# A new order of the work and a fourth place for the inner sums in a two-layer graph network on one core

## The chip, the cores and the metric

The kernel runs on one core of a Trainium2 chip. The core's engines are TensorE (PE in the profile; its weight loads are shown apart as PEld), VectorE (DVE), ScalarE (ACT), GpSimd (POOL) and SyncE (SP), whose queue issues nearly all the transfers here. The metric is the device time of one execution in microseconds (us). A single run is named with its own time, several runs with their median.

## The reference, cut to what matters

There are 128 graphs of 128 nodes with 512 features each, and two layers. All is float32.

```python
deg  = sum(adj, -1, keepdims=True)                      # layer 0
agg  = einsum('bij,bjf->bif', adj, x) / maximum(deg, 1e-6)
x    = layernorm(x + relu(concat([x, agg], 2) @ W.T))

Xw   = x @ Wv + bv                                      # layer 1
sj, si = Xw @ aw[:d, 0], Xw @ aw[d:, 0]
a    = adj * exp(leaky_relu(sj[:, None, :] + si[:, :, None] + ab, 0.2))
T    = a / (sum(a, -1, keepdims=True) + 1e-12)
H    = (x @ Wk[0] + bk[0]) + T @ ((x @ Wk[1] + bk[1]) + T @ (x @ Wk[2] + bk[2]))   # same sum, regrouped
out  = layernorm(x + relu(H))
```

(The reference writes H as a loop over k with powers of T; the kernel computes the nested form in the last line but one. How the biases of the second and first term pass through T is folded into constants made once at the start.)

## The kernel before

Work goes in groups of four graphs: 32 groups in layer 0, then 32 in layer 1. A group is a matrix of 512 rows by 512 features. It is multiplied by a wide matrix of weights (1024 columns in layer 0, 4 x 385 in layer 1, the two score columns among them) by a scheme of seven products in place of eight, used on two levels: seven outer products of seven inner ones each, so 49 products of 128x128 weights with 256 or 385 columns. The sums and differences that such a scheme needs are made by GpSimd on the left operands, and by VectorE and ScalarE when they take results out of the accumulators.

The accumulators are eight PSUM banks, `bA` and `bB`, in two lanes of four. An outer product takes a lane for seven steps. Seven steps of one outer product are chained: the first is copied to another bank (so the third, which adds to the same bank, must wait for that copy), the third is added to a saved sum (so the fifth must wait for that addition), and so on. To hide these waits the steps of two outer products, one in each lane, are interleaved.

Names of steps, as they stand in the strings of the program and in the text below: in layer 0 `P12`, `P56` and `P74` are pairs of outer products (a step is two products, 0.86 us), `t.1` to `t.7` are the inner steps of the last outer product and `t.8` to `t.11` the four products with the normalised adjacency; a small first letter (`p74`) means the group before. In layer 1 `O1` to `O7` are outer products (a step is one product of 385 columns, 0.65 us) and `c.1` to `c.8` are the T products of `combine` for the group before (0.86 us each, 512 columns); `x.1` to `x.8` are those of the very last group. Each graph b of a group has two T products. `one(b)` multiplies T with the third term, adds the second term (two VectorE additions, lines 829 and 830) and puts this inner sum into a place `v1s`, and then ScalarE copies the first term into the bank (line 831). `two(b)` multiplies T with the inner sum on top of that copy, and `residual` (line 380) takes the bank out, with ReLU, residual and the row sum for the layer norm. There are three places for inner sums.

The order is written by hand, or rather by tables. `PA`, `PB` and their like give the order of the steps on TensorE: `PF` for the first group, `PA` for a group of layer 0, `PT` and `PG` at the passage to layer 1, `PB` for a group of layer 1, `PL` for the last one. The tables `PLACES_...` give, for all other work (loads, transpositions, sums, layer norm, softmax, stores), the half step after which it is issued. A function issues its instructions where its place stands, and every engine runs its own instructions in that order, so the tables decide also what stands in front of what in the queues of VectorE, ScalarE, GpSimd and SyncE. Semaphores guard the data; an early place never makes a wrong result, and a late or a crowded one makes a wait.

Lines that the text needs: 155 (all products), 259 (transposition of the left operand, 0.6 to 0.7 us on VectorE), 400 and 401 (sums of `t.2`), 409 (sum of `t.5`), 599 and 601 (degree), 614 and 810 (transposition of the adjacency or of T), 626 (bias copied into a bank before `O5.1`), 637 and 676 (additions that the fifth and the seventh step of an outer product wait for), 504 and 517 (ScalarE's two passes of the layer norm), 725 to 734 (scores), 784 to 802 (softmax of the scores), 744 to 770 (the last group's softmax, which makes the row sums on TensorE and keeps T in place of the detour through memory that the other groups take).

```python
for f, b in ((one, 0), (one, 1), (one, 2), (two, 0), (one, 3), (two, 1), (two, 2)):
    f(b)
    yield
two(3)
```

Of the kernel before, what the change touches and what calls it, by code (L numbers as in the profile page):

```python
# [8 lines left out]
FP = mybir.dt.float32  # L9
# [7 lines left out]
def kernel(  # L17
# [15 lines left out]
    P = 128  # L33
# [25 lines left out]
    def need(*keys):  # L59
        for k in keys:  # L60
            assert k in done, k
# [10 lines left out]
    v1s = [big[:, 28 * BW + F * i : 28 * BW + F * (i + 1)] for i in range(3)]  # L72
# [78 lines left out]
    for t in bA + bB:  # L151
        nc.tensor.matmul(t, ident, ident[:, None, :].to_broadcast([P, Q, P]), start=True, stop=True)
# [603 lines left out]
    def end_rows(g, h):  # L756
        need(("end_scores", g), ("adj_turn",))
        T = TTs[g][:, 2 * h : 2 * h + 2].rearrange("p b n -> p (b n)")
        pt = lanes[0][1 + h][:, :FH]
        V.tensor_mul(T, T, adjs[2 * NG - 1][:, 2 * h : 2 * h + 2].rearrange("p b n -> p (b n)"))  # L760
        mm(pt, ones[:].to_broadcast([P, P]), T, True)

    def end_norm(g, h):
        need(("end_rows", g, h))
        T = TTs[g][:, 2 * h : 2 * h + 2].rearrange("p b n -> p (b n)")
        pt = lanes[0][1 + h][:, :FH]
        rr = halves()[:, :FH]
        V.tensor_scalar(rr, pt, ROW_EPS, None, ALU.add)
        V.reciprocal(rr, rr)  # L769
        V.tensor_mul(T, T, rr)  # L770
# [41 lines left out]
    def combine(lane, g):  # L812
        n = NG + g
        X, Y, W, Z = lane
        at_ = {0: X, 1: Z, 2: W, 3: Y}
# [8 lines left out]
        def one(b):  # L824
            need(("end_norm", g, b // 2) if g == NG - 1 else ("t_turn", g))
            need(("O4" if b > 1 else "O3", g, 7), ("sum_c", g, 0), ("sum_c", g, 1))
            mm(at_[b], TTs[g][:, b], row(b, 0, F, 0), True)
            v = v1[b] = v1s[(g * G + b) % 3]
            V.tensor_add(v[:, :258], at_[b][:, :258], row(b, F, 2 * BW, 0))
            V.tensor_add(v[:, 258:], at_[b][:, 258:], row(b, 0, 254, 1))  # L830
            L_.copy(at_[b], row(b, 254, 766, 1))  # L831

        def two(b):
            mm(at_[b], TTs[g][:, b], v1[b])
            late.append((residual, n, b, at_[b]))
        for f, b in ((one, 0), (one, 1), (one, 2), (two, 0), (one, 3), (two, 1), (two, 2)):
            f(b)
            yield
# [12 lines left out]
    def step(lane, name, g, k):  # L851
# [3 lines left out]
    PA = "p74.5 P12.1 P12.2 p74.6 P12.3 p74.7 P12.4 t.1 P12.5 P12.6 t.2 P12.7 P56.1 t.3 P56.2 t.4 t.5 P56.3 t.6 t.7 t.8 t.9 t.10 t.11 P74.1 P74.2 P56.4 P56.5 P56.6 P74.3 P56.7 P74.4".split()  # L855
    PT = "p74.5 p74.6 O1.1 O1.2 O1.3 p74.7 O1.4 t.1 O1.5 O1.6 t.2 O1.7 O2.1 t.3 O2.2 t.4 t.5 O2.3 t.6 t.7 t.8 t.9 t.10 t.11 O2.4 O2.5 O2.6".split()
    PG = ("O5.1 O5.2 O5.3 O5.4 O2.5 O2.6 O6.1 O6.2 O5.5 O5.6 O5.7 O7.1 O6.3 O6.4 O7.2 "
          "O6.5 O2.7 O7.3 O6.6 O7.4 O6.7 O4.1 O4.2 O7.5 O4.3 O7.6 O7.7 O4.4 c.1 O4.5 "
          "O4.6 c.2 c.3 c.4 O4.7 O3.1 O3.2 O3.3 O3.4 c.5 c.6 c.7 c.8 O3.5 O3.6").split()
    PB = ("O1.1 o3.7 O1.2 O1.3 O2.1 O1.4 O1.5 O1.6 O2.2 O1.7 O2.3 O2.4 O5.1 O5.2 O2.5 O5.3 O2.6 O5.4 O2.7 "  # L860
          "O6.1 O5.5 O6.2 O5.6 O6.3 O5.7 O6.4 O7.1 O6.5 O6.6 O7.2 O7.3 O6.7 O4.1 O7.4 O7.5 O4.2 O4.3 O7.6 "
          "O4.4 O4.5 O7.7 c.1 O4.6 O4.7 O3.1 O3.2 c.2 O3.3 c.3 c.4 c.5 c.6 c.7 c.8 O3.4 O3.5 O3.6").split()
    PL = ("O1.1 o3.7 O1.2 O2.1 O1.3 O2.2 O1.4 O1.5 O1.6 O1.7 O2.3 O2.4 O5.1 O2.5 O5.2 O2.6 O2.7 O5.3 O5.4 O6.1 O5.5 O6.2 "
# [44 lines left out]
    def place_op(n, pos, name, m, *a):  # L908
# [7 lines left out]
        ("ln_apply", -2, 3): 4, ("ln_var", -2, 0): -9, ("sum_c22", -2): -40, ("ln_scales", -2): -1, ("ln_mean", -2): -15,  # L916
        ("ln_var", -2, 2): -4, ("load_y", -2, 1): -27, ("ln_apply", -2, 2): 10, ("ln_var", -2, 1): -4,
        ("load_y", -2, 0): -31, ("x_s4", -1): -36, ("ln_var", -2, 3): -12, ("x_s1", -1): -66, ("a_load", -2): -65,
        ("a_turn", -2): -36, ("x_s3", -1): -52, ("y_store", -2, 1): 25, ("ln_apply", -2, 1): 15, ("x_turn", 0, 0, 1): -20,
        ("y_store", -2, 0): 32, ("ln_apply", -2, 0): 15, ("load_left", 0, 0): -49, ("ln_apply", -1, 3): 68, ("x_s2", 0): 28,  # L920
        ("x_turn", 0, 1, 1): -37, ("load_adj", 0): 154, ("ln_var", -1, 0): 58, ("sum_c22", -1): 21, ("ln_scales", -1): 62,
        ("ln_mean", -1): 48, ("x_turn", 0, 0, 0): -28, ("ln_var", -1, 2): 55, ("load_y", -1, 1): 38, ("load_y", -1, 0): 40,
        ("ln_var", -1, 1): 55, ("ln_apply", -1, 2): 70, ("x_s1", 0): 5, ("x_turn", 0, 1, 0): -39, ("a_load", -1): 7,
        ("x_turn", 1, 0, 1): 55, ("x_inner", 0, 0): -12, ("a_norm", -1): -23, ("ln_var", -1, 3): 58, ("degree", -1): -48,
        ("a_turn", -1): 27, ("x_s3", 0): 19, ("y_store", -1, 1): 95, ("ln_apply", -1, 1): 79, ("x_inner", 0, 1): -29,
        ("y_store", -1, 0): 100, ("ln_apply", -1, 0): 82, ("load_left", 1, 0): 9, ("x_s1", 1): 97, ("x_turn", 1, 0, 0): 41,
        ("x_s2", 1): 99, ("x_s4", 0): 80, ("load_left", 1, 1): -24, ("x_inner", 1, 1): 61, ("x_turn", 1, 1, 0): 32,
        ("x_s3", 1): 127, ("x_inner", 1, 0): 64, ("x_turn", 1, 1, 1): 47, ("x_s2", -1): -44,
    }
    PLACES_A = {  # L930
        ("x_s4", 0): 35, ("ln_apply", 0, 3): 131, ("x_s2", 1): 86, ("x_turn", 1, 1, 1): 33, ("ln_var", 0, 0): 124,
        ("sum_c22", 0): 87, ("ln_scales", 0): 126, ("w_slot", 0, 1): 24, ("ln_mean", 0): 113, ("x_turn", 1, 0, 0): 33,
        ("ln_var", 0, 2): 124, ("load_y", 0, 1): 100, ("ln_var", 0, 1): 118, ("load_y", 0, 0): 100, ("ln_apply", 0, 2): 134,
        ("x_s1", 1): 67, ("x_turn", 1, 1, 0): 28, ("a_load", 0): 73, ("x_inner", 1, 0): 51, ("a_norm", 0): 36,
        ("ln_var", 0, 3): 115, ("degree", 0): 17, ("load_left", 2, 1): 38, ("w_slot", 0, 0): 4, ("a_turn", 0): 90,
        ("x_s3", 1): 83, ("y_store", 0, 1): 157, ("ln_apply", 0, 1): 140, ("x_turn", 1, 0, 1): 42, ("x_inner", 1, 1): 36,
        ("load_adj", 1): 37, ("y_store", 0, 0): 161, ("ln_apply", 0, 0): 138, ("load_left", 2, 0): 78,
    }
    PLACES_B = {
        ("t_norm", 0): 154, ("sum_r", 0, 1): 81, ("load_y", 0, 0): 170, ("ln_var", 0, 3): 230, ("x_turn", 1, 0, 1): 19,  # L940
        ("t_back", 0): 165, ("x_s1", 1): 66, ("ln_scales", 0): 239, ("t_sums", 0): 149, ("x_turn", 1, 1, 1): 19,
        ("load_left", 2, 0): 82, ("ln_var", 0, 1): 227, ("y_store", 0, 0): 264, ("t_turn", 0): 187, ("ln_var", 0, 2): 224,
        ("sum_c", 0, 0): 109, ("ln_apply", 0, 2): 273, ("ln_apply", 0, 3): 257, ("x_inner", 1, 1): 53, ("ln_var", 0, 0): 235,
        ("t_exp", 0): 140, ("load_left", 2, 1): 70, ("ln_apply", 0, 1): 257, ("y_store", 0, 1): 278, ("x_s2", 1): 68,
        ("x_turn", 1, 1, 0): -5, ("x_s3", 1): 97, ("ln_apply", 0, 0): 242, ("t_load", 0): 123, ("t_scores", 0): 119,
        ("x_turn", 1, 0, 0): 14, ("sum_r", 0, 0): 86, ("x_s4", 0): 42, ("load_adj", 0): 103, ("load_y", 0, 1): 190,
        ("ln_mean", 0): 223, ("sum_c", 0, 1): 115, ("x_inner", 1, 0): 41,
    }
    PLACES_M = {
        ("ln_mean",): 212, ("ln_apply", 3): 234, ("ln_var", 1): 219, ("ln_apply", 0): 250, ("y_store", 0): 251,  # L950
        ("ln_apply", 2): 231, ("ln_var", 2): 225, ("ln_apply", 1): 235, ("ln_var", 3): 225, ("ln_scales",): 230,
        ("y_store", 1): 244, ("ln_var", 0): 227,
    }
    PLACES_L = {
        ("end_store", 2): 158, ("sum_c", 1): 72, ("sum_r", 0): 71, ("end_store", 0): 158, ("t_scores",): 105,
        ("end_var", 1): 134, ("sum_r", 1): 71, ("load_adj",): 96, ("load_y", 0): 47, ("end_apply", 1): 160,
        ("load_y", 1): 106, ("end_mean", 1): 128, ("end_rows", 0): 111, ("end_mean", 0): 127, ("end_rstd", 2): 132,
        ("end_store", 1): 160, ("end_apply", 2): 137, ("end_stats", 2): 129, ("end_store", 3): 162, ("end_scales",): 140,
        ("sum_c", 0): 76, ("end_rstd", 3): 149, ("end_apply", 0): 144, ("end_scores",): 106, ("end_rows", 1): 111,
        ("end_norm", 0): 111, ("end_stats", 3): 138, ("end_norm", 1): 111, ("end_apply", 3): 158, ("adj_turn",): 96,  # L960
        ("end_var", 0): 131,
# [118 lines left out]
```

## Time and profile before

| what | us |
|---|---|
| median of 3 runs | 2085.56 (2084.93 to 2086.3) |
| the profiled execution, its own time | 2083.08 |
| its span, first to last instruction | 2081.3 |
| a group of layer 0, start to start in the chain of waits (101.57 to 126.32) | 24.75 |
| a group of layer 1 (919.52 to 958.43) | 38.91 |
| TensorE busy from 60 to 790 | 730.00 of 730 |
| TensorE busy from 860 to 2040 | 1179.80 of 1180 |
| TensorE busy from 2051.00 to 2072.70, the last group's end | 16.80 of 21.70 |
| after the last product, to the end of the span | 8.60 |

A page of this profile shows busy time by engine, the chain of work that ended last, and groups of instructions. A view of waits adds up, for one engine, the idle time before its instructions and what ended it. A timeline gives start, duration, engine, line, operation, tiles (written <- read), shapes and, in brackets, idle time before the instruction and what ended it. Each float32 product stands there as two weight loads and two MATMUL records, one after the other.

### The profile page before, as it was taken

How to read it: one execution, taken by the hardware profiler on the slowest of the kernel's cores; microseconds unless marked ns; L12 is line 12 of the kernel's file. 1: busy time of each engine (PE TensorE's matmuls, PEld its weight loads, DVE VectorE, ACT ScalarE, POOL GpSimd, SP SyncE). 2: the span in 40 equal slices, each digit the busy share in tenths (PEclk: the TensorE clock that was granted, in tenths of full speed). 3: DMA queues.
4: the chain of work that ended last, by engine and by line, in shares of the span. 5: the costliest groups of instructions: out<-in, count | busy, mean ns of one | idle time of the engine just before them, and what ended most of it. 6: DMA issues, size and time to landing. Idle time of an engine off the chain costs nothing.

```text
span 2081.3 us, 25875 instructions
## 1 busy us (share of the span) xinstructions
PE 2062.5 (99%) x7096; PEld 1329.9 (64%) x7096; DVE 1525.8 (73%) x3414; ACT 1155.7 (56%) x2875; POOL 1377.7 (66%) x1263
## 2 busy tenths in 40 slices
PE   9999999999999999999999999999999999999997
PEld 6778888888878886555555555555555555555553
DVE  6777777777777777676776776776776776776766
ACT  2656666666666666355455455455455465465464
POOL 5877888887676776656656656656556556556552
PEclk9999999999999999999999999999999999999999
DMA  9776666666667776435434535535535435435423
GB/s 206 174 190 194 180 182 179 160 187 192 163 160 190 190 183 218 107 87 122 116 87 115 124 87 127 112 87 128 111 87 130 109 87 132 107 87 132 107 67 117
DMA packets 431070, 287.13 MB, mean 138 GB/s; under 512 B 155593, under 2 KB 353865, under 8 KB 430924
## 3 DMA queue, kind: packets, MB, share of 16 engines
q1 hardware_dynamic: 429996, 284.15, 54.6%
q10 hardware_dynamic: 800, 1.31, 0.3%
q8 instruction: 56, 0.92, 0.2%
q14 instruction: 90, 0.74, 0.1%
q0 software_dynamic: 128, 0.01, 0.0%
HBM read 191.60 MB, written 93.79 MB: 137 GB/s over the span
## 4 chain that ended last, share of the span: by engine, by line
PE 97%; DVE 1%; DMA 1%; ACT 0%; issue 0%; POOL 0%; SPq 0%; ACTq 0%; DVEq 0%
PE bA L155 51%; PE bB L155 46%; DMA yd<-y 0%; DMA xb<-in_x_dram 0%; DMA y<-in_x_dram 0%; PE bA L181 0%; DVE s L769 0%; DVE y L380 0%; POOL r L709 0%; ACT y L517 0%; DVE big L995 0%; DVE xl L259 0%; DVE xu L259 0%; DVE big L1003 0%; SPq L83 0%
## 5 line engine op out<-in xcount | busy, mean ns | idle before, releaser
L155 PE MATMUL bB<-big,xu 128*128 128x385 f32 (+1 forms) x1806 | 569.5, 435 | 1.0 <-DVE c L676 0.7
L155 PEld LDWEIGHTS bB<-big,xu 128*128 128x128 f32 x1806 | 339.4, 190 | 166.6 <-issue 30.1
L155 PE MATMUL bA<-big,xl 128*128 128x256 f32 (+1 forms) x1358 | 395.9, 416 | 0.3 <-DVE bA L475 0.3
L155 PE MATMUL bB<-big,xs 128*128 128x256 f32 (+1 forms) x1316 | 388.8, 416 | 0.0
L155 PEld LDWEIGHTS bA<-big,xl 128*128 128x128 f32 x1358 | 256.8, 189 | 100.1 <-issue 15.5
L155 PEld LDWEIGHTS bB<-big,xs 128*128 128x128 f32 x1316 | 249.5, 190 | 84.2 <-issue 1.7
L155 PE MATMUL bA<-big,xu 128*128 128x256 f32 (+1 forms) x896 | 290.0, 435 | 0.2
L155 PE MATMUL bA<-c,TT 128*128 128x512 f32 x512 | 245.9, 592 | 3.0 <-DVE c L669 1.9
L504 ACT ACTIVATE junk<-y,mv 128x512 bf16<-128x512 f32 x252 | 181.3, 719 | 72.7 <-POOL mv L499 68.5
L155 PEld LDWEIGHTS bA<-big,xu 128*128 128x128 f32 x896 | 165.4, 189 | 82.2 <-DVE bA L637 9.7
L517 ACT ACTIVATE y<-y,mv,rstd 128x512 f32<-128x512 f32 x252 | 201.5, 812 | 1.4 <-POOL mv L512 1.4
L380 DVE SCALAR_TENSOR_TENSOR y<-bA,y 128x512 f32<-128x512 f32 x256 | 170.4, 683 | 19.6 <-PE bA L155 13.4
L155 PE MATMUL bA<-big,xs 128*128 128x385 f32 x448 | 178.3, 492 | 0.0
L709 POOL TENSOR_TENSOR r<-r,s 128x770 f32<-128x770 f32 x64 | 115.1, 1820 | 86.4 <-DVE c L669 86.4
L155 PE MATMUL bB<-big,xl 128*128 128x385 f32 (+1 forms) x462 | 167.2, 480 | 0.5 <-ACT bA L456 0.4
L155 PEld LDWEIGHTS bA<-c,TT 128*128 128x128 f32 x512 | 96.8, 189 | 93.0 <-issue 48.1
L790 POOL TENSOR_TENSOR T<-ag,T 128x512 f32<-128x512 f32 x31 | 39.5, 1275 | 175.9 <-ACT T L785 175.9
L499 POOL TENSOR_SCALAR mv<-mv 128x4 f32<-128x4 f32 x63 | 14.5, 230 | 212.3 <-DVE y L380 212.3
L270 POOL TENSOR_TENSOR xs<-xl 128x896 f32<-128x896 f32 x63 | 131.4, 2086 | 23.9 <-PE bB L155 23.9
L282 POOL TENSOR_TENSOR xu<-xu,xs 128x896 f32<-128x896 f32 x63 | 131.8, 2091 | 8.8 <-PE bB L155 8.8
L831 ACT COPY bA<-r 128x512 f32<-128x512 f32 x64 | 37.7, 590 | 176.4 <-DVE big L830 170.7
L637 DVE TENSOR_TENSOR bB<-bB,s 128x385 f32<-128x385 f32 x128 | 72.5, 567 | 85.1 <-PE bB L155 75.4
(190 smaller groups left out, 3636.7 us busy)
## 6 DMA issues: line engine op xcount, KB each, us to landing
xb<-in_x_dram SPq DMA_DIRECT2D x256, 128.0 KB, 3.8
y<-in_x_dram SPq DMA_DIRECT2D x64, 512.0 KB, 4.3
yd<-y SPq DMA_DIRECT2D x64, 512.0 KB, 3.0
xb<-yd SPq DMA_DIRECT2D x256, 128.0 KB, 5.8
y<-yd SPq DMA_DIRECT2D x64, 512.0 KB, 5.9
out_dram<-y SPq DMA_DIRECT2D x62, 512.0 KB, 2.8
ag<-in_adj_dram SPq DMA_DIRECT2D x63, 256.0 KB, 5.9
sb<-sd SPq DMA_DIRECT2D x252, 64.0 KB, 3.2
```

The lines of the kernel that those rows point to most:

```text
L155: nc.tensor.matmul(dst, lhsT, rhs, start=start, stop=True, skip_group_check=True)
L270: S_.tensor_add(xs[n][:, 0], xl[n][:, 0], xl[n][:, 1])
L282: S_.tensor_sub(xu[n][:, 1], xu[n][:, 1], xs[n][:, 1])
L380: V.scalar_tensor_tensor(y, t, 0.0, y, ALU.max, ALU.add, accum_out=mvs[n][:, b, 0:1])
L499: S_.tensor_scalar(mvs[n][:, :, 0], mvs[n][:, :, 0], -1.0 / F, None, ALU.mult)
L504: L_.activation(junk, ys[n, b // 2][:, b % 2], AF.Square, bias=mvs[n][:, b, 0:1], accum_out=mvs[n][:, b, 1:2])
L517: L_.activation(y, y, AF.Identity, bias=mvs[n][:, b, 0:1], scale=rstds[n][:, b : b + 1])
L637: V.tensor_add(W, X, s5)
L709: S_.tensor_add(r, r, s)
L790: S_.tensor_mul(T, adjs[NG + g], T)
L831: L_.copy(at_[b], row(b, 254, 766, 1))
```

## The change

1. `v1s` has a fourth place, a tile of its own, and each graph has its own place. In `combine` all four `one` stand ahead of the four `two`, in all groups but the last, where the order stays as it was.
2. The last group. The row sums of its softmax are made as columns: four products with a vector of ones in place of two with a matrix of ones. The reciprocal is then taken of two numbers in each row in place of 256, spread to a diagonal, and brought back to all rows by a product with ones. For three of its four graphs the first term is no longer copied by ScalarE: a product with the identity puts it into a bank of the other lane ahead of time (`end_base`), and the second T product goes there.
3. One of the eight warm-up products at the start is left out.
4. The strings `PA`, `PT`, `PG`, `PB` and `PL`, and all tables of places apart from that of the start, have new values.

```diff
-    v1s = [big[:, 28 * BW + F * i : 28 * BW + F * (i + 1)] for i in range(3)]
+    v1s = [big[:, 28 * BW + F * i : 28 * BW + F * (i + 1)] for i in range(3)] + [const.tile([P, F], FP, name="v1x")]
...
-    for t in bA + bB:
+    for t in bA + bB[:3]:
...
     def end_rows(g, h):
-        need(("end_scores", g), ("adj_turn",))
+        need(("end_scores", g), ("adj_turn",), *[("end_rows", g, 0)] * h)
+        T, pt = TTs[g], lanes[0][0]
+        t2 = T[:, 2 * h : 2 * h + 2].rearrange("p b n -> p (b n)")
+        V.tensor_mul(t2, t2, adjs[2 * NG - 1][:, 2 * h : 2 * h + 2].rearrange("p b n -> p (b n)"))
+        for b in (2 * h, 2 * h + 1):
+            mm(pt[:, b : b + 1], T[:, b], ones, b == 0)
+
+    def end_recip(g, h):
+        need(("end_rows", g, 1))
+        t = lanes[0][0][:, 2 * h : 2 * h + 2]
+        rr = small.tile([P, 2], FP, name="rr2")
+        V.tensor_scalar(rr, t, ROW_EPS, None, ALU.add)
+        V.reciprocal(rr, rr)
+        if h == 0:
+            ends["dr"] = p1.tile([P, G, N], FP, name="dr", tag="sb")
+        for b in (0, 1):
+            V.tensor_scalar(ends["dr"][:, 2 * h + b], ident, rr[:, b : b + 1], None, ALU.mult)
+
+    def end_norm(g, h):
+        need(("end_recip", g, 1), *[("end_norm", g, 0)] * h)
         T = TTs[g][:, 2 * h : 2 * h + 2].rearrange("p b n -> p (b n)")
-        pt = lanes[0][1 + h][:, :FH]
-        V.tensor_mul(T, T, adjs[2 * NG - 1][:, 2 * h : 2 * h + 2].rearrange("p b n -> p (b n)"))
-        mm(pt, ones[:].to_broadcast([P, P]), T, True)
-
-    def end_norm(g, h):
-        need(("end_rows", g, h))
-        T = TTs[g][:, 2 * h : 2 * h + 2].rearrange("p b n -> p (b n)")
-        pt = lanes[0][1 + h][:, :FH]
-        rr = halves()[:, :FH]
-        V.tensor_scalar(rr, pt, ROW_EPS, None, ALU.add)
-        V.reciprocal(rr, rr)
-        V.tensor_mul(T, T, rr)
+        pt = lanes[0][0][:, h * FH : (h + 1) * FH]
+        mm(pt, ones[:].to_broadcast([P, P]), ends["dr"][:, 2 * h : 2 * h + 2].rearrange("p b n -> p (b n)"), h == 0)
+        V.tensor_mul(T, T, pt)
+
+    def end_base(g, b):
+        need(("sum_c" if b > 1 else "O3", g, 0 if b > 1 else 7))
+        t = (rs[NG + g], last22[g])[b // 2][:, b % 2].rearrange("p n m -> p (n m)")
+        mm(lanes[0][1 + b], ident, t[:, 254:766], True)
...
-        at_ = {0: X, 1: Z, 2: W, 3: Y}
+        at_ = to = {0: X, 1: Z, 2: W, 3: Y}
+        if g == NG - 1:
+            to = {0: lanes[0][1], 1: lanes[0][2], 2: lanes[0][3], 3: X}
...
-            v = v1[b] = v1s[(g * G + b) % 3]
+            v = v1[b] = v1s[b]
...
-            L_.copy(at_[b], row(b, 254, 766, 1))
+            if g < NG - 1 or b == 3:
+                L_.copy(to[b], row(b, 254, 766, 1))
...
-        for f, b in ((one, 0), (one, 1), (one, 2), (two, 0), (one, 3), (two, 1), (two, 2)):
+        x, y = ((two, 0), (one, 3)) if g == NG - 1 else ((one, 3), (two, 0))
+        for f, b in ((one, 0), (one, 1), (one, 2), x, y, (two, 1), (two, 2)):
...
-    PA = "... P12.4 t.1 P12.5 P12.6 t.2 P12.7 P56.1 t.3 P56.2 t.4 t.5 P56.3 t.6 t.7 ... P74.1 P74.2 P56.4 P56.5 P56.6 P74.3 P56.7 P74.4".split()
+    PA = "... t.1 P12.4 P12.5 t.2 P12.6 P12.7 P56.1 t.3 P56.2 t.4 t.5 P56.3 t.6 t.7 ... P74.1 P56.4 P74.2 P56.5 P56.6 P74.3 P56.7 P74.4".split()
...
-    PB = ("... O2.3 O2.4 O5.1 O5.2 O2.5 O5.3 O2.6 O5.4 O2.7 "
-          "O6.1 O5.5 O6.2 O5.6 O6.3 O5.7 O6.4 O7.1 ... "
-          "O4.4 O4.5 O7.7 c.1 O4.6 O4.7 O3.1 O3.2 c.2 O3.3 c.3 c.4 c.5 c.6 c.7 c.8 O3.4 O3.5 O3.6").split()
+    PB = ("... O2.3 O2.4 O5.1 O5.2 O2.5 O5.3 O2.6 O5.4 O5.5 "
+          "O2.7 O6.1 O5.6 O6.2 O6.3 O5.7 O6.4 O7.1 ... "
+          "O4.4 O4.5 O7.7 O4.6 c.1 O4.7 O3.1 c.2 c.3 O3.2 c.4 c.5 c.6 O3.3 c.7 c.8 O3.4 O3.5 O3.6").split()
```

In `PLACES_B` the last pass of the layer norm, `ln_apply`, moves among others (graph 1 from 257 to 262, graph 2 from 273 to 276), one `y_store` (278 to 284), `x_turn` of the second half of the first two graphs (19 to 29), and the scores and the softmax, by 2 or 3 half steps each.

## The prediction

> **What bounds the kernel now.** I read the page's busy times and chain first, then TensorE's weight-load waits, then timelines of one group of each layer and of the end.
>
> ```profile
> PE 2062.5 (99%) x7096; PEld 1329.9 (64%) x7096; DVE 1525.8 (73%) x3414; ACT 1155.7 (56%) x2875; POOL 1377.7 (66%) x1263
> PE 97%; DVE 1%; DMA 1%; ACT 0%; issue 0%; POOL 0%; SPq 0%; ACTq 0%; DVEq 0%
> ```
>
> TensorE sets the time: the change can only remove products (one, 0.86 us) or delays of products. Work elsewhere counts only through what a product waits for. But a busy 100% hides delays: a late product's record is simply drawn longer. So the weight loads' waits say more (total us, times, longest):
>
> ```profile
> PEld bA L155 <- ACT bA L831: 23.8, 37, 1.6
> PEld bB L155 <- DVE r L676: 14.1, 30, 0.8
> PEld bA L155 <- DVE bA L637: 10.3, 31, 0.6
> PEld bA L155 <- DVE s L401: 8.8, 31, 0.3
> ```
>
> 30 or 31 times means once in every group. These are idle times of the loader, not losses: a load normally starts 0.2 to 0.3 before its product is due. The loss shows at the product. Layer 0, `t.3`:
>
> ```profile
> 541.51 0.59 PE L155 MATMUL bA<-big,xu 128*128 128x256 f32 x2
> 542.32 0.16 DVE L599 TENSOR_REDUCE deg<-deg 128x4 f32<-128x8 f32 x1 [0.62 <-ACT junk L597]
> 543.25 0.41 DVE L401 TENSOR_TENSOR s<-bA,s 128x256 f32<-128x256 f32 x1
> 543.71 0.30 PEld L155 LDWEIGHTS bA<-big,xu 128*128 128x128 f32 x2 [0.29 <-DVE s L401]
> 543.71 0.70 PE L155 MATMUL bA<-big,xu 128*128 128x256 f32 x2
> ```
>
> `t.2`'s record is 0.59 long, `t.3`'s 0.70 because its load starts with it: 0.104 lost, and the steps after lose 0.05. 31 x 0.154 = 4.8 us. VectorE had stood 0.62 at the degree's L599 with L400 and L401 behind it. Layer 1, `c.8` and `o3.7`, then `O1.5`:
>
> ```profile
> 1624.40 0.30 PEld L155 LDWEIGHTS bA<-big,TT 128*128 128x128 f32 x2 [0.63 <-ACT bA L831]
> 1627.39 0.52 DVE L676 TENSOR_TENSOR r<-bB,r 128x385 f32<-128x385 f32 x1
> 1627.96 0.30 PEld L155 LDWEIGHTS bB<-big,xu 128*128 128x128 f32 x2 [0.46 <-DVE r L676]
> 1627.97 0.92 PE L155 MATMUL bB<-big,xu 128*128 128x385 f32 x2
> ...
> 1592.26 0.98 PEld L155 LDWEIGHTS bA<-big,xu 128*128 128x128 f32 x4 [0.32 <-DVE bA L637]
> ```
>
> `o3.7` is 0.92 against the usual 0.81: 0.11. `c.8` starts 0.074 late, its load having a lead of about 0.04. `O1.5` (load 1592.26, product due 1592.39: lead 0.13) loses nothing. I use this scale: lead 0.13 or more costs 0; 0.04 to 0.06, some 0.05 to 0.07; none, 0.10 to 0.11, plus all lateness.
>
> The end (TensorE's waits; one line of the timeline):
>
> ```profile
> PE bA L155 <- DVE c L669: 1.9, 1, 1.9
> PE bA L155 <- DVE TT L770: 1.0, 1, 1.0
> PE bA L155 <- ACT bA L831: 0.8, 1, 0.8
> ...
> 2060.43 1.75 DVE L769 RECIPROCAL s<-s 128x256 f32<-128x256 f32 x1
> ```
>
> Here the softmax is on the path: TensorE works 16.80 of 21.70 us.
>
> [...] the trace has 1.75 us for 256 columns where the addition of the same size takes 0.42. [...] here 0.16 to 0.18 for 4 columns (L599, L601).
>
> **The change part by part.** "Due" is where the product would start with no wait; from a product's end to VectorE's start is 0.20 in the trace, from VectorE to a load 0.05.
>
> 1. *Layer 0.* `t.1` and `t.2` stand one step of 0.86 earlier, so three P steps lie between `t.2` and `t.3`; on VectorE L400 and L401 now come ahead of L599 and L601. `t.3`'s delay goes: -4.8, of which I keep 0.2 for steps near it: **-4.6**. Next late is `t.7`, whose L409 comes behind L404 (0.47 to the next), L614 and an L259: I find its end 0.17 to 0.24 before `t.7` is due, so free. If the lead is gone: 31 x 0.10 = +3.2 (bounds 0 to 3.2).
>
> 2. *`combine`.* With four places `one(3)` no longer waits for `two(0)`, and its copy L831 is done over 1.5 us before `c.8`: 30 x 0.074 = **-2.2**. The place itself costs no time. `o3.7` keeps its wait: the chain from `c.8`'s end is 0.20, residual 0.72, L669 0.47, L259 0.63, L676 0.52, then 0.05: 2.59 to 2.60 against 2.585 for four steps of 0.647. The residual of `c.8` starts 0.02 later: 30 x 0.02 = **+0.6** (bounds -3.3, wait gone, to +3).
>
> 3. *`O5.5`* is moved ahead of `O2.7` and `O6.1`, and one L259 (place 19 to 29) now stands ahead of its L637. From before's times: L676 starts 1598.58, +0.47, +0.63 for L259, +0.53 for L637, +0.05 = 1600.26 against 1600.32 due: lead 0.06, so 30 x 0.05 = **+1.5** (bounds 0 to 30 x 0.11 = 3.3).
>
> 4. *`O5.1`* loses 0.16 a group: its bias copy L626 starts 1595.71, behind an L517 (0.71 to 0.81) and an L634. The same operations stand ahead of it after: **0** (bounds -2.6, if the 0.085 of lateness goes, to +2).
>
> 5. *Softmax chain, moved later.* ScalarE now runs an L504 (0.73) ahead of the scores and an L517 ahead of L784. The whole chain shifts by 0.7 to 0.75: SP's L736 and L777 (1593.71 to 1594.4; landing in at most 3.2 by the page of T, so by 1597.7), L784 1597.66 to 1598.4, GpSimd's L790, VectorE's L792, ScalarE's L802 (four, 1.27), SP's L586 and the two `sb` loads to 1606.6 (landing 1611.9), T's transposition at about 1614.2, against `one(0)` over 4 us later. What stands behind L802: L634 for `O6.3`, then L637 at about 1605.05 to 1605.62, against `O6.5` due 1606.14, a lead of 0.46, 0.34 more than the 0.13 needed: **0**. One `y_store` goes behind the `sb` loads in SP's queue; the `y` load then lands about 1617.7, needed 1623.5: 0.
>
> 6. *The last group.* `c.4` waited 0.95 for ScalarE's L831 behind VectorE's additions; these come earlier: -0.95; `c.8` -0.08. From the end of `c.8` (2051.00): seven O steps to `O4.4` 4.53; the scores' product waits for L730 till 4.86 and takes 0.96; `O4.5` 0.65, to 6.47; two identity products (`end_base`) 1.72, to 8.19; row sums wait for the second L760 (8.56), then eight passes at 0.11 (starts of two loads: 0.30 less 0.19), to 9.15 rounded up; `O4.6`, third identity product, normalising product 0.43, `O4.7`, another 0.43, VectorE's multiplication partly beside them: `x.1` at 12.17 (before 11.70). The long reciprocals (twice 0.42 + 1.75 + 0.42) shrink to a few operations of 0.16 to 0.21. Then eight T products without a wait, 6.87 (before 9.95). Tail 9.0 (before 8.65: I add 0.35 for residuals closer together). Sum 28.0 against 30.3, so -2.3 - 1.03, rounded: **-3.2** (bounds -4.2 to -2).
>
> 7. *Warm-up product.* The first product of the work proper waits for VectorE's L995, which ends 1.1 after the warm-up does (12.39, 11.31): **0**.
>
> 8. *Passage between layers.* About 2.9 us are lost there, most of it at `O2.7` and around residuals that wait for loads of `y`; order changes, loads don't: **+0.2** (±1).
>
> Sum: -4.6 - 2.2 + 0.6 + 1.5 - 3.2 + 0.2 = -7.7. The profiled execution, 2083.08 (span 2081.3 and 1.78 around it), becomes 2075.4; it was 2.5 below the median, so the median 2085.56 becomes 2077.9, said as 2078.0.
>
> **The rivals.** 0.2% is 4.2 us, about what a measurement of this kernel can tell from no change: below 2081.4 is faster, above 2089.7 slower.
>
> - *As summed*, 2074 to 2082: chance 0.50 (0.47 faster, 0.03 same).
> - *More gain.* `O5.5` is free (-1.5), `o3.7` no worse (-0.6), `O5.1`'s lateness goes (30 x 0.085 = -2.6): -12.4, 2073.2. For it: these are queues in which 0.05 decides, and all three waits have ScalarE or VectorE work ahead that moves. Against: I find the same operations ahead of L626. 0.17, all faster.
> - *Less gain: the near waits come in full.* `t.7` +3.2, `O5.5` +1.8 more: -2.7, 2082.9. For it: `t.7`'s lead (0.17) and `O5.5`'s (0.06) are worked out from starts of other groups. 0.19 (0.03 faster, 0.16 same).
> - *Slower: the softmax chain slips in front of L634.* If T's load lands 1.45 later than I take it (SP's queue holds loads ahead of it), L784 starts 0.75 later still, and L802 pushes L634 and L637 past `O6.5`'s lead: (0.75 - 0.34 + 0.10) x 30 = +15.3, 2093.2. It costs from a slip of 0.34, and the kernel is slower than before from about 0.5. For it: the longest chain through memory has been moved by its whole margin. Against: 0.7 of margin at L784. 0.14, slower.
>
> Faster 0.47 + 0.17 + 0.03 = 0.67, same 0.03 + 0.16 = 0.19, slower 0.14. The range 2071 to 2087 holds the first three with the bounds of `o3.7` and `O5.1`, and the smaller slips of the last; about 0.15 is left out.
>
> **What would show it.** Right: no load wait on L401 is left; the wait on the copy of the first term (L831 of before) falls to a few us; `o3.7`'s wait on L676 stays near 14 us in 30; a wait on L637 at `O5.5` is new; at the end the waits of 1.9 and 1.0 go. Layer 0's group falls from 24.75 to 24.60, layer 1's stays within 0.05 of 38.91. Wrong: a group of layer 0 that stays at 24.7 or more (a next wait took over), a group of layer 1 at 39.1 or more with waits on L637 at `O6.5` or on T, or an end as long as before.

## The result, and the profile after

| | before | after |
|---|---|---|
| median, us | 2085.24 | 2074.34 (2074.15 to 2074.61) |
| ratio, 95% interval | | 0.9946 [0.993, 0.9962] |
| profiled execution, and its span | 2083.08, 2081.3 | 2074.15, 2072.4 |
| a group of layer 0, mean of 29 (`p74.5` to `p74.5`) | 24.75 | 24.63 |
| a group of layer 1, mean of 30 (`O1.1` to `O1.1`) | 38.92 | 38.92 |
| first group of layer 1, `O5.1` to the next `O1.1` | 25.11 | 23.15 |

The kernel after is faster by 10.9 us at the medians (of four executions each) and by 8.9 in the profiled executions. What the other 2 us most likely are is told in the last section. First, of TensorE's weight-load waits in the kernel after, the largest that end with the work of another engine (total us, times, longest):

```profile
PEld bA L155 <- ACT bA L849: 15.8, 63, 0.8
PEld bB L155 <- DVE r L676: 14.2, 30, 0.8
PEld bA L155 <- DVE bA L637: 12.5, 32, 0.4
PEld bA L155 <- DVE c L669: 7.2, 30, 0.2
PEld bA L155 <- DVE bA L397: 4.8, 29, 0.5
```

L401 is gone. L637 is now that of `O5.5`, once a group; before, the same name stood for the harmless one at `O1.5`. L849 is the copy that was L831; its 15.8 looks like a wait that stayed, but 63 waits of 0.25 are only the loader's usual lead, and no T product of the 30 groups is late by them. So sums of this view mislead in both directions. I therefore measured losses at the products: the distance from the start of one MATMUL record to the next, less the usual 0.216, 0.323 or 0.429 us for 256, 385 or 512 columns. "Loses" below means this.

The timeline of layer 0, after (start, duration, engine, line, operation):

```profile
537.36 0.42 DVE L397 TENSOR_TENSOR bA<-bA,s 128x256 f32<-128x256 f32 x1
537.84 0.30 PEld L155 LDWEIGHTS bA<-big,xu 128*128 128x128 f32 x2 [0.15 <-DVE bA L397]
537.92 0.61 PE L155 MATMUL bA<-big,xu 128*128 128x256 f32 x2
...
539.07 0.41 DVE L401 TENSOR_TENSOR s<-bA,s 128x256 f32<-128x256 f32 x1
...
540.03 0.16 DVE L599 TENSOR_REDUCE deg<-deg 128x4 f32<-128x8 f32 x1 [0.55 <-ACT junk L597]
...
540.97 0.59 PE L155 MATMUL bA<-big,xu 128*128 128x256 f32 x2
```

`t.3` (540.97) comes 1.5 us after its sum L401, and the degree stands behind it. In exchange `t.2` (537.92) comes close behind L397: its load starts only 0.08 before it, and 0.02 is lost inside `t.2`, in all 0.7 us, and another 0.3 us in all just ahead of it. Layer 1, after, at `O5.5`:

```profile
1592.79 0.70 DVE L259 STREAM_TRANSPOSE xu<-xb 128x512 f32<-128x512 f32 x1
1593.42 0.54 DVE L637 TENSOR_TENSOR bA<-bA,s 128x385 f32<-128x385 f32 x1
...
1594.01 0.30 PEld L155 LDWEIGHTS bA<-big,xs 128*128 128x128 f32 x2 [0.40 <-DVE bA L637]
```

`O5.5` loses 0.055 in each group behind that L259. The passage between the layers, before, then after (SPq is SyncE's queue, L576 the last store of `y`, L95 the loads of `y`, L380 a residual, L676 the addition that `O2.7` waits for):

```profile
813.39 0.38 SPq L576 DMA_DIRECT2D yd<-y  x1
814.27 6.02 SPq L95 DMA_DIRECT2D y<-in_x_dram  x2
821.28 0.69 DVE L380 SCALAR_TENSOR_TENSOR y<-bA,y 128x512 f32<-128x512 f32 x1 [2.37 <-DMA y<-in_x_dram]
826.69 0.56 DVE L676 TENSOR_TENSOR c<-bB,c 128x385 f32<-128x385 f32 x1
827.30 0.92 PE L155 MATMUL bB<-big,xu 128*128 128x385 f32 x2 [0.69 <-DVE c L676]
```

```profile
809.17 0.37 SPq L576 DMA_DIRECT2D yd<-y  x1
810.88 3.60 SPq L95 DMA_DIRECT2D y<-in_x_dram  x2
815.47 0.69 DVE L380 SCALAR_TENSOR_TENSOR y<-bA,y 128x512 f32<-128x512 f32 x1 [0.58 <-PE bA L155]
817.64 0.52 DVE L676 TENSOR_TENSOR c<-bB,c 128x385 f32<-128x385 f32 x1
```

The second load of `y` is issued 0.37 before the end of the L95 entry: 819.92 before, 6.5 us after the store, whose buffer it takes; 814.11 after, 4.9 us after it. Before, the first residual waited for that load and everything behind it on VectorE was late; after, it waits for its product.

In the last group the waits of 1.9, 1.0, 1.0 and 0.8 us are gone. From the end of `c.8` to `x.1` it is 12.53 us (11.69 before), from `x.1` to the start of `x.8` 6.01 (8.81), from there to the span's end 10.08 (9.80); the T products ahead of `O4.1` save 1.17. Together -2.8.

### The profile page after: what moved, and what is told of

Same layout as the page of the kernel before. It is cut to its first block, busy times and chain, and to the rows that moved or that the text cites. A ratio compares the mean times of both kernels' runs of the same rounds, so it can differ in the third digit from the quotient of the medians.

```text
span 2072.4 us, 25921 instructions
## 1 busy us (share of the span) xinstructions
PE 2058.1 (99%) x7108; PEld 1334.0 (64%) x7108; DVE 1528.7 (74%) x3418; ACT 1158.7 (56%) x2872; POOL 1377.4 (66%) x1263
## 4 chain that ended last, share of the span: by engine, by line
PE 58%; DVE 0%; POOL 0%; issue 0%; ACT 0%; ACTq 0%; DVEq 0%
PE bA L155 31%; PE bB L155 27%; DVE y L380 0%; ACT y L562 0%; POOL rs L539 0%; DVE st L546 0%; ACTq L1097 0%; DVE xl L259 0%; DVE dg L730 0%; DVE r L669 0%; POOL rs L555 0%; DVE r L676 0%; POOL mv L499 0%; POOL mv L540 0%; POOL ve L538 0%
## 5 line engine op out<-in xcount | busy, mean ns | idle before, releaser
L155 PE MATMUL bA<-big,xl 128*128 128x256 f32 (+1 forms) x1358 | 405.9, 416 | 0.3 <-DVE bA L475 0.3
L504 ACT ACTIVATE junk<-y,mv 128x512 bf16<-128x512 f32 x252 | 181.8, 721 | 122.6 <-POOL mv L499 112.4
L155 PE MATMUL bA<-c,TT 128*128 128x512 f32 x512 | 240.8, 592 | 0.0
L517 ACT ACTIVATE y<-y,mv,rstd 128x512 f32<-128x512 f32 x252 | 205.2, 816 | 3.8 <-POOL mv L512 1.7
L380 DVE SCALAR_TENSOR_TENSOR y<-bA,y 128x512 f32<-128x512 f32 x253 | 168.0, 682 | 11.7 <-PE bA L155 6.4
L155 PE MATMUL bB<-big,xl 128*128 128x385 f32 (+1 forms) x462 | 172.1, 480 | 0.4 <-ACT bA L456 0.4
L637 DVE TENSOR_TENSOR bB<-bB,s 128x385 f32<-128x385 f32 x128 | 72.6, 567 | 130.6 <-ACT s L634 50.3
L849 ACT COPY bA<-r 128x512 f32<-128x512 f32 x62 | 36.6, 590 | 190.4 <-DVE big L847 149.8
L669 DVE TENSOR_TENSOR r<-bB,r 128x385 f32<-128x385 f32 x192 | 106.5, 555 | 43.9 <-PE bB L155 40.0
```

Of the source, the lines that this page charges most:

```text
L155: nc.tensor.matmul(dst, lhsT, rhs, start=start, stop=True, skip_group_check=True)
L380: V.scalar_tensor_tensor(y, t, 0.0, y, ALU.max, ALU.add, accum_out=mvs[n][:, b, 0:1])
L504: L_.activation(junk, ys[n, b // 2][:, b % 2], AF.Square, bias=mvs[n][:, b, 0:1], accum_out=mvs[n][:, b, 1:2])
L517: L_.activation(y, y, AF.Identity, bias=mvs[n][:, b, 0:1], scale=rstds[n][:, b : b + 1])
L637: V.tensor_add(W, X, s5)
L669: V.tensor_add(part(dst, b, BW), t, part(src, b, BW))
```

## The experiments

| run | median | ratio to the kernel before (run beside it), 95% interval |
|---|---|---|
| e1_degree | 2088.17 | 1.0017 [1.0009, 1.0024] |
| e2_weights | 2084.29 | 1.0001 [0.9992, 1.0009] |
| e3_passage | 2087.81 | 1.0015 [1.0008, 1.0022] |
| e4_two_first | 2075.12 | 0.9957 [0.9942, 0.9972] |
| e5_degree_sum | 2085.74 | 1.0004 [0.9995, 1.0012] |
| e6_turn_behind | 2072.84 | 0.9943 [0.9928, 0.9958] |
| e7_long_recip | 2075.52 | 0.9956 [0.9941, 0.997] |
| e8_base_copy | 2079.26 | 0.9972 [0.9962, 0.9982] |
| e9_order_a | 2087.34 | 1.0013 [1.0006, 1.002] |
| e10_queues | 2064.41 | 0.9902 [0.9888, 0.9917] |
| e11_old_loads | 2074.82 | 0.9952 [0.9935, 0.9968] |
| e12_places_a | 2115.38 | 1.0148 [1.0131, 1.0165] |

The runs of the kernel before spread from 2082.58 to 2086.7, so a median tells little below 1 us; the losses of one step in the traces repeat within about 0.1 us per 30 groups. So the experiments are judged by the losses.

**Layer 0: what frees `t.3`?**

```diff
-("degree", 0): 17
+("degree", 0): 21
```

> The kernel before with one edit: in layer 0 the degree stands two steps later (place 17 becomes 21), so that VectorE runs the two sums of t.2 (L400, L401) ahead of the degree's L599 and L601; the order on TensorE stays. Theory A, the gain of layer 0 is made in VectorE's queue: t.3 loses nothing, a group of layer 0 falls from 24.75 to about 24.60, 31 groups give -4.6 us, median about 2080.6. Rival B, it is made by TensorE's order (t.1 and t.2 one step forward): the group stays at 24.75, median 2085.2.

Neither. `t.3` loses nothing, as theory A says, but layer 0 is slower by 3.3 us: `t.4` loses 0.27 a group. The weight loads now wait for L404:

```profile
PEld bA L155 <- DVE bA L404: 12.6, 31, 0.5
```

ScalarE's inputs of the degree (L597) moved too, and L599 now waits for them (0.52) in front of L404. So I moved only VectorE's part:

```diff
 def degree(g):            # L597 x4 stay at place 17
...
+def degree_sum(g):        # reduction and reciprocal, place 21
```

> The kernel before with one edit: only the two small operations of the degree on VectorE (its reduction and its reciprocal) stand behind L400 and L401; their four inputs on ScalarE (L597) stay where they were, so that nothing on VectorE waits for them. Theory A (VectorE's queue sets layer 0, and the first try moved the wait to t.4 only because ScalarE's part moved too): t.3 and t.4 lose nothing, a group of layer 0 takes 24.60 in place of 24.75, -4.6 us, median 2080. Rival B (the third step between t.2 and t.3 on TensorE is needed): 0.05 to 0.15 a group stays at t.3, median above 2082.

Theory A falls: layer 0 loses 5.8 us (5.5 before). The timeline of this kernel:

```profile
542.13 0.19 ACT L597 ACTIVATION_READ_ACCUMULATOR junk<-ag 128x1 f32 x1
542.22 0.62 ACT L343 COPY r<-bB 128x256 f32<-128x256 f32 x2
542.61 0.43 DVE L344 TENSOR_TENSOR c<-bB,r 128x256 f32<-128x256 f32 x1 [0.88 <-ACT r L343]
...
543.28 0.41 DVE L401 TENSOR_TENSOR s<-bA,s 128x256 f32<-128x256 f32 x1
...
543.75 0.30 PEld L155 LDWEIGHTS bA<-big,xu 128*128 128x128 f32 x2 [0.29 <-DVE s L401]
```

With L599 gone, L344 stands in front of the sums and waits (0.88), for a ScalarE copy L343 that stands behind the four L597. With L597 moved too (e1_degree) `t.3` was free, with L599 alone it is not: the first cause is on ScalarE; L599 was only the nearest of two operations that wait for it. Then the order alone, and the places alone:

```diff
-PA = "p74.5 P12.1 P12.2 p74.6 P12.3 p74.7 P12.4 t.1 P12.5 P12.6 t.2 P12.7 ...
+PA = "p74.5 P12.1 p74.6 P12.2 P12.3 p74.7 t.1 P12.4 P12.5 t.2 P12.6 P12.7 ...
```

> The kernel before with one edit: the string PA of the kernel after, so that in layer 0 t.1 and t.2 stand a step earlier; all places stay as before, so that the degree (L599, L601) still stands ahead of L400 and L401 on VectorE. Theory B (TensorE's order frees t.3, since its two sums then have a third step of 0.86 us to cover them, whatever stands ahead of them): t.3 loses nothing, t.2 loses 0.02 as in the kernel after, a group takes 24.62, -3.9 us, median 2081. Theory A (the place of the degree ahead of the sums matters): 0.1 or more a group stays at t.3 or t.4; median 2084 or more.

```diff
-PLACES_A = { ... values of before
+PLACES_A = { ... values of after
```

> The kernel before with one edit: the table PLACES_A of the kernel after; the string PA stays as before. With e9_order_a this takes the change of layer 0 apart. Theory (order and places of layer 0 work only together): with the old order the degree's four inputs L597 fall behind a copy L343 that waits for P12.6, L599 and L601 wait for them, and L400 and L401 stand behind those; from the times of e1_degree L401 would then end about 1.2 us after t.3 is due, so that each of some 30 groups loses about 1.2 us: +35 us, median 2120. Rival (the places alone bring the gain of layer 0, as they free ScalarE ahead of L397): -3 us or more, 2082 or less.

Losses of layer 0: before 5.5, order alone 8.5, places alone 37.9, both (the change) 1.6 us. With the order alone `t.3` is free, as theory B says, but `t.2` loses 0.26 a group:

```profile
541.43 0.36 ACT L364 COPY c<-bA 128x256 f32<-128x256 f32 x1
...
542.29 0.42 DVE L366 TENSOR_TENSOR c<-bA,c 128x256 f32<-128x256 f32 x1
542.63 0.42 DVE L397 TENSOR_TENSOR bA<-bA,s 128x256 f32<-128x256 f32 x1
...
543.11 0.30 PEld L155 LDWEIGHTS bA<-big,xu 128*128 128x128 f32 x2 [0.40 <-DVE bA L397]
543.11 0.70 PE L155 MATMUL bA<-big,xu 128*128 128x256 f32 x2
```

L364 comes late, behind passes L517 of the layer norm (0.81 to 0.82 each), and L365, L366 and L397 follow it back to back. With the places alone it is `t.3`, by 1.2 us a group:

```profile
563.77 0.16 DVE L599 TENSOR_REDUCE deg<-deg 128x4 f32<-128x8 f32 x1 [1.17 <-ACT junk L597]
...
564.37 0.41 DVE L401 TENSOR_TENSOR s<-bA,s 128x256 f32<-128x256 f32 x1
...
564.84 0.70 PE L155 MATMUL bA<-big,xu 128*128 128x256 f32 x2 [0.95 <-DVE s L401]
```

Two halves, each of which alone makes layer 0 slower, make the gain.

**The passage.**

```diff
-PLACES_T = { ... values of before     (loads of layer 1's weights)
+PLACES_T = { ... values of after
```

> The kernel before with one edit: the loads of layer 1's weights stand in the places that the change gives them; one of the three that stood between the last stores of y moves ahead of them. The first group of layer 1 lost 2.5 us before and 0.5 after. Theory A, the gain at the passage is made by the transfers: the last store of y of layer 0's group 30 lands in 5 us in place of 6.5, the second load of y starts over 1 us earlier, the loss ahead of O2.7 (0.86 and what follows it) goes, the first group of layer 1 gains 2.0 us, and the median falls to about 2083 or lower, since the runs of the kernel before are 2 us longer than its profiled execution while those of the kernel after are not. Rival B, it is made by the order of PT and PG: nothing changes at O2.7, median 2085.2.

The first group of layer 1 takes 23.87 in place of 25.11: -1.2 of the 2.0. The second load of `y` follows the store by 5.2 us in place of 6.5, and the loss ahead of `O2.7` is gone. At the median this can't be told from the spread, and the idea that the kernel before has a load that varies between runs got no support (the last section shows what does vary).

```diff
-PT = "... t.5 O2.3 t.6 t.7 t.8 t.9 t.10 t.11 O2.4 O2.5 O2.6"
+PT = "... t.5 t.6 O2.3 t.7 t.8 O2.4 O2.5 t.9 O2.6 t.10 t.11"
...
(PG as after; the layer norm's places of layer 0's last group too)
```

> The kernel before with the change's strings PT and PG, and the places that go with them for the layer norm of the last group of layer 0; loads and stores stay as before. Rival B of the run before: with O2.4 and O2.5 earlier, L676 of O2.5 stands ahead of the last three residuals on VectorE, so O2.7 doesn't wait: first group of layer 1 gains 2.0 us, median about 2083. Theory A: the loads of y come as late as before, the first residual waits about 1.9 us for one, what stands behind it on VectorE is late, and half or more of the 2.5 us stays: median 2084.5 to 2085.5.

27.12 us, 2.0 more than before. `O5.2` waits for a residual, and `O5.3` for a copy that waits for another, 1.8 together: the load of `y` came late as before, over 6 us after the store. Another 2.05, at `O7.3`, is a wait that this mixture made itself, on a copy behind two passes of the layer norm:

```profile
PE bA L155 <- ACT bA L628: 2.5, 2, 1.8
```

(The other of the two is that of `O5.3`.) Taking these 2.05 off, 25.07 is left, as before: by this sum the order alone gives nothing. The next group loses another 1.4 ahead of `O1.5`, for L637, which I didn't follow. The counter-test:

```diff
-PLACES_T = { ... values of after
+PLACES_T = { ... values of before
```

> The kernel after with one edit: the loads of layer 1's weights stand where they stood before. Theory A (the transfers made the gain at the passage): the last store of y takes over 6 us again, the second load of y comes 1 us or more later, the first residual waits for it, and the first group of layer 1 and the passage lose 1 to 2 us; median 2075.5 to 2076.5. Rival B (in the order of the kernel after, with the last residuals behind L676, the loads don't matter): within 0.3 us in the first group; median 2074.3.

Between the two: 23.68 (after 23.15), 0.3 of it between `O2.7` and `O5.3`; the second load of `y` follows the store by 5.7 us. The last group of layer 0 loses 0.6 more, which I didn't follow. So the loads' order makes more than half of the gain in the first group when added to before (1.2 of 2.0), and a quarter when taken from after (0.5): with the rest of the change the chain has some room. How the rest splits between the order and the moved loads of `y` was not tried.

**Layer 1.**

```diff
-x, y = ((two, 0), (one, 3)) if g == NG - 1 else ((one, 3), (two, 0))
+x, y = ((two, 0), (one, 3)) if True else ((one, 3), (two, 0))
```

> The kernel after with one edit: in every group the second product of graph 0 stands ahead of the first product of graph 3 again, as before; the four places and all orders stay. Theory A, the order of the T products took away the wait of c.8: it comes back, 0.07 a group, +2.2 us, 2076.5. Rival B, it is the step O3.3 that now lies between c.6 and c.7, which gives the copy of graph 3's first term 0.65 us more: c.8 loses nothing, 2074.3.

Rival B: `c.8` loses nothing in all 30 groups (1167.65 us for them, 1167.68 after). All first products ahead of the second are not needed there. What frees it is the step `O3.3` between `c.6` and `c.7`: in the kernel before and here the copy of graph 3's first term ends 2.49 us after the start of that graph's first product, but it ends 0.08 ahead of `c.8` there and 0.73 ahead here, and the difference is that step's 0.65. The copy and `c.8` in this kernel:

```profile
1617.70 0.59 ACT L849 COPY bA<-c 128x512 f32<-128x512 f32 x1 [1.36 <-PE bA L155]
...
1619.02 1.02 PE L155 MATMUL bA<-v1x,TT 128*128 128x512 f32 x2
```

The order of the T products is worth 0.9 us once, in the last group, where they follow each other without such a step.

```diff
-("x_turn", 1, 0, 1): 29
+("x_turn", 1, 0, 1): 31
```

> The kernel after with one edit: the transposition L259 of x_turn (second half, second place) stands one step later (place 29 becomes 31), behind the addition L637 that O5.5 waits for. Theory A: the 0.055 that O5.5 loses in each group is this L259 in front of it; it goes, 30 x 0.055 = -1.6 us, a group of layer 1 takes 38.87 in place of 38.92, median 2072.7. Rival B: O5.5 stands too close to O5.3 in any case (L632 and L676 ahead of L637), 0.03 or more stays; median 2073.5 or more.

Theory A: `O5.5` loses nothing, 30 groups take 1166.06, -1.6. Then all three waits of layer 1 at once, with four places:

```diff
-("x_turn", 1, 0, 1): 29, ("x_turn", 1, 1, 0): -5, ("ln_apply", 0, 0): 242, ("ln_apply", 0, 3): 256
+("x_turn", 1, 0, 1): 31, ("x_turn", 1, 1, 0): 1, ("ln_apply", 0, 0): 252, ("ln_apply", 0, 3): 264
```

> The kernel after with four places of layer 1 changed, each to take one operation out from in front of an operation that a product waits for: x_turn (second half, second place) behind L637 for O5.5 (29 to 31), x_turn (-5 to 1) behind L676 for o3.7, the first L517 of the layer norm behind the bias copy L626 for O5.1 (242 to 252), and the third L517 out of the way of the softmax (256 to 264). If the three waits are what stands in front of those operations and nothing else, they go: 30 x (0.105 + 0.159 + 0.055) = -9.6 us, a group of layer 1 takes 38.60, median 2064.8. Rival: the operations moved back hold up what comes next on their engines (L637 for O1.5, L628 for O5.3, the softmax), and a third to a half comes back: 2068 to 2070.

The first: 30 groups take 1157.72, 10.0 less than after, 38.59 each; the median is 2064.41, 0.5% below the kernel after and 1% below the one before. No wait for L676 or L637 that comes once in every group is left. The largest that are:

```profile
PEld bA L155 <- ACT bA L849: 15.8, 63, 0.8
PEld bA L155 <- DVE c L669: 7.2, 30, 0.2
PEld bA L155 <- ACT an L606: 7.2, 30, 0.2
PEld bA L155 <- DVE bA L416: 7.0, 29, 0.2
PEld bA L155 <- DVE bA L397: 4.3, 26, 0.5
```

Nothing that was moved back held up anything else: in these groups no step loses more than 0.01 on average.

**The end.**

```diff
-mm(pt[:, b : b + 1], T[:, b], ones, b == 0)
+mm(pt, ones[:].to_broadcast([P, P]), T, h == 0)
...
-rr = small.tile([P, 2], FP, name="rr2")
+rr = halves()[:, :FH]
...
-mm(pt, ones[:].to_broadcast([P, P]), ends["dr"] ..., h == 0)
-V.tensor_mul(T, T, pt)
+V.tensor_mul(T, T, ends["rr", h])
...
(places of the reciprocals and of the multiplications of T, by one half step)
```

> The kernel after, with the row sums and reciprocals of the last group's softmax as before: two products with a matrix of ones, additions, reciprocals and multiplications of 256 columns, no diagonal and no product that brings it back; the order of the T products, the products with the identity and the fourth place stay. Theory A, the short reciprocals made the gain of the end: the first eight T products wait again, by 2 us or more; median 2076.5. Rival B, the gain of the end came from the bases that no longer wait for ScalarE and from the order of the work, and the long reciprocals, which run beside O4.6, a base and O4.7, cost little: 0.3 to 1 us; median 2075.

Between the two: from the end of `c.8` to the end of the span 1.25 us more, with two waits of TensorE again:

```profile
PE bA L155 <- DVE c L669: 1.1, 1, 1.1
PE bA L155 <- DVE TT L773: 0.9, 1, 0.9
```

So the short reciprocals, with the products that go with them, are somewhat less than half of the end's 2.8. With the 0.9 of e4_two_first that is 2.1; the rest was not taken apart.

```diff
-mm(lanes[0][1 + b], ident, t[:, 254:766], True)
+L_.copy(lanes[0][1 + b], t[:, 254:766])
...
(row sums, reciprocals and multiplications of T one or two half steps later)
```

> The kernel after with the three products with the identity replaced by copies on ScalarE into the same banks, between its passes of the layer norm, and the row sums placed behind O4.6, which they would otherwise hold up. Theory A, the three products (2.6 us) lie beside waits for the softmax only in part: TensorE then waits for the row sums by about 1.2 us, and x.1 starts 0.6 to 1.1 us earlier; median 2073.5. Rival B, they are hidden by those waits: x.1 starts where it does now, 12.35 us after c.8's end, or later; median 2074.3 or more.

(The `x.1` at 12.35 in this expectation should read 12.53. The kernel leaves part of the result out, probably some of the first term of three graphs, which was not followed up; the operations that run are those named.) It says nothing on the identity products: the diagonal L773 waited 2.05 us, the profile names a pass L504 behind the copies, and TensorE stood 2.33 us. What came then is told in the last section. Whether the three products are worth their 2.6 us stays open.

## Why the prediction was right or wrong

| step | predicted | measured in the profiled executions |
|---|---|---|
| 1, layer 0 | -4.6 | -3.9 |
| 2, `c.8` | -2.2 | -2.2 |
| 2, `o3.7` | +0.6 | 0.0 |
| 3, `O5.5` | +1.5 | +1.6 |
| 4 and 5, `O5.1`, softmax chain | 0 | 0.0 |
| layer 1, other steps | | +0.6 |
| 6, the last group | -3.2 | -2.8 |
| 7, warm-up, with all up to the second group | 0 | -0.3 |
| 8, passage | +0.2 | -2.0 |
| sum (measured: of unrounded values) | -7.7 | -8.9 |

The sign, the range and the likeliest case were right; the time was 3.7 us too high, from two places. (The -0.3 of step 7 says nothing: in the profiles of the kernels here that stretch lies between 36.98 and 38.17 us.)

- *Step 8 failed* where it says "order changes, loads don't". They did: the loads of the weights moved in SyncE's queue, the last store of `y` came free of one of them, and the load that waits for its buffer came 1.6 us sooner. The diff showed the table; I read it as having no consumer near.
- *The step from the profiled execution to the median.* I carried the 2.5 us between them over to the new kernel (2075.4 to 2077.9). The new kernel's profiled execution lies 0.2 below its median; that of before was at the low end of its own spread. This spread has a cause, most likely TensorE's clock in the last group (last section), which goes with the waits there: four executions of the kernel after spread over 0.5 us. By this estimate some 2 of the 10.9 us are a gain that no step of the sum holds. Against 2074.15 the sum for the profiled execution was 1.3 too high.
- *Step 1*: the size was near, the account half right. That `t.7` would be next in line was wrong (0.1 us in all); it was `t.2`, whose cover shrank by the same move that widened that of `t.3`. And the queue that I blamed, VectorE's with L599, was only where ScalarE's lateness showed.
- *Step 2*: right size, wrong cause: not the places and the order of the T products, but the step `O3.3` between them. The fourth place itself costs nothing, as said: products that read it take 592 ns, as those that read the others do. And the sign that was named for it failed: the wait on the copy fell to 15.8 us and not to a few, without a loss behind it. `o3.7` is as late as before; 0.02 of a chain added from typical starts is below what such a sum can tell.
- *Step 3* is the best one: a lead of 0.06 read from before, priced at 0.05, measured 0.055. The scale of leads and losses, from three waits of before, held.
- *Step 5*: the softmax chain moved later and cost nothing; the margin that I computed was there (L637 ends 0.59 ahead of `O6.5`, 0.52 in the sum).
- *Step 6*: the sum promised 0.4 too much. `x.1` came at 12.53 and not 12.17, late at the two normalising products and ahead of them; the T products took their 6.87 (6.01 and one step of 0.86); from the start of `x.8` to the end it was 10.08 and not 9.86; and the T products ahead of `O4.1` saved 1.17 and not 1.03.

The +0.6 in layer 1 is 0.5 ahead of one `O1.7`, in the second group, and small change; it was in no step.

## What to carry to other kernels

Price a wait at the consumer, not in the view of waits: how late does the product start, and how much lead did its load have? In a dense, in-order schedule look through the operation that waits to the first late one (here ScalarE's L597 behind L599 and L344), and when a step moves forward, ask which wait behind it loses its cover. An operation that nobody needs soon and that stands in front of one a product waits for is worth a search by itself: four such places gave about as much as the whole change. And where a median moves by more than the losses in the traces explain, look at the clock of each execution (here a mean of 0.997 in the 15 longest of 93, 0.998 or more in the 20 shortest).

## What the runs showed of the hardware

In e8_base_copy TensorE ran at half its clock (0.50 granted) after the wait. The busy time by stretch (window: length, busy time of PE, PEld, DVE, ACT and POOL with their instructions, then the granted clock of TensorE, the DMA share and GB/s):

```profile
2054.00:2056.50 2.50, 0.26 (x1) 0.00 (x0) 0.54 (x3) 1.93 (x6) 0.41 (x2) 0.87 0.00 0
2056.50:2058.00 1.50, 1.22 (x2) 0.50 (x2) 0.83 (x5) 0.33 (x1) 1.06 (x2) 0.50 0.00 0
...
2061.00:2062.00 1.00, 1.00 (x3) 0.43 (x2) 0.70 (x2) 0.00 (x0) 0.00 (x0) 0.50 0.00 0
2062.00:2063.00 1.00, 1.00 (x3) 0.43 (x2) 0.14 (x2) 0.59 (x1) 0.00 (x0) 0.67 0.00 0
```

Taken as either 1.00 or 0.50, the clock fell some 1.6 us into the wait of 2.33 us (0.87 is the mean from 2054.00 to 2056.50) and came back between 2062 and 2063 (mean 0.67), some 6 us after work resumed at 2056.59: about 6.8 us at half clock. The products without a wait between them took longer: from `x.1` to the start of `x.4` it took 4.23 us in place of 2.58.

The same fall stands in the profiles of e1_degree, e9_order_a and e12_places_a, and there no wait is as long: their last group is that of the kernel before, with its waits of 1.9, 1.0, 1.0 and 0.8 us. The two products behind the wait of 1.9, in the kernel before:

```profile
2065.74 1.98 PE L155 MATMUL bA<-c,TT 128*128 128x512 f32 x4 [1.92 <-DVE c L669]
```

and in e1_degree, with the clock around them:

```profile
2068.40 3.78 PE L155 MATMUL bA<-c,TT 128*128 128x512 f32 x4 [1.93 <-DVE c L669]
...
2066.00:2067.00 1.00, 0.47 (x2) 0.00 (x0) 1.00 (x1) 0.00 (x0) 0.00 (x0) 1.00 0.00 0
2068.00:2069.00 1.00, 0.60 (x1) 0.50 (x2) 1.00 (x3) 0.00 (x0) 0.00 (x0) 0.50 0.00 0
```

From `x.1` to the start of `x.8` it is 11.36 us in e1_degree, 10.00 in the other two, and 8.81 in the kernel before, whose clock is at 1.00 until its products are done. So the same waits stand in profiles with the fall and in one without it. The longest wait in the last group is 2.33 us in e8_base_copy and 1.9 us in the other three; that these waits bring the clock down is my reading of when it fell, and no run here shows what else decides.

This is most likely why the runs of the kernel before spread. Of its 93 executions beside the experiments, all 15 at or above 2085.8 us had a mean granted clock of 0.997, and none of the 20 at or below 2083.5 had less than 0.998. The profiled executions with that end and a full clock (before, e2_weights, e3_passage, e5_degree_sum; mean 0.998 to 0.999) lie 1.4 to 2.4 us below the medians of their kernels, the three with a fall (0.997 to 0.998) 0.1 below to 0.8 above. The kernel after spreads over 0.5 us. No profile of the kernel before itself shows the fall while it works, so this stays an inference. In e8_base_copy the wait of 2.33 us was not the whole cost: another 1.65 us went between `x.1` and `x.4` at half clock.
